# Neighbouring rows by a copy inside SBUF instead of two transposes: a four-layer residual kernel on one core of Trainium2

## The chip, the cores and the metric

The kernel runs on one core of one Trainium2 chip. The core has five engines, each with its own instruction queue: TensorE (PE in the profile; its weight loads are PEld), VectorE (DVE), ScalarE (ACT), GpSimd (POOL) and SyncE (SP). SP computes nothing here; it issues the DMA transfers. Engines wait for each other, and for transfers, through semaphores. The metric is device microseconds (us) of one execution; the result of a kernel is the median of its runs.

## The reference

The input x has 128 examples of 128 rows and 512 features (float32). Four layers follow, and each adds its result to x. All depend on per-example numbers (a mask kind, a language, three factors, a category).

```python
# layer 0: attention pooling with a mask per example
x = x + _L0_cond_ref(x, W1, b1, v, itok_B_0_2)
# layer 1: adapter with the language's weights, then a layer norm
x = x + _L1_cond_ref(x, itok_B_0_8, W1, b1, W2, b2, gamma, beta)
# layer 2: y is x after layer 1
yp_x = jnp.pad(y, ((0, 0), (0, 0), (1, 1)), mode='reflect')
lap_x = (yp_x[:, :, :-2] - 2.0 * y + yp_x[:, :, 2:]) / (dx * dx)
yp_y = jnp.pad(y, ((0, 0), (1, 1), (0, 0)), mode='reflect')
lap_y = (yp_y[:, :-2, :] - 2.0 * y + yp_y[:, 2:, :]) / (dy * dy)
du_dt = zX * lap_x + zY * lap_y + zR * y * (1.0 - y)      # factors of the example
x = x + du_dt
# layer 3: one 512x512 matrix per category
x = x + einsum('bsd,bdh->bsh', x, W[cat]) + b[cat][:, None, :]
```

The change touches layer 2. For each value it needs the neighbouring rows (`lap_y`) and the neighbouring features (`lap_x`), reflected at the edges.

## The kernel before, in words

One example is one tile of work: 128 rows on 128 partitions, 512 features along the row. Layers 0 and 1 run in this layout. For layer 2 the example is turned, because layer 3 needs the features on the partitions: partition p then holds features 4p to 4p + 3, as four chunks of 128 rows. In this layout

- the neighbouring rows of a value lie beside it on the same partition;
- the neighbouring features of chunks 1 and 2, and one neighbour each of chunks 0 and 3, lie in another chunk of the same partition;
- the feature before chunk 0 is chunk 3 of partition p - 1, and the feature after chunk 3 is chunk 0 of partition p + 1. These two are called the outer planes.

`y_transpose` (L514) turns the example by four TensorE transposes into `tr_y` (L524) and makes the two outer planes by two more, shifted by one feature, into `tr_e` (L528). `planes` (L530) copies all six into one SBUF tile `yT` of six planes with a border column at each side: the four inner ones (L534), the outer two (L535), the border columns (L536). `neighbours` (L545, GpSimd) adds the rows above and below into `ud`; `side_neighbours` (L553, GpSimd) adds the planes to the left and right into `lr`; `own` (L538, ScalarE), `diffuse_own`, `diffuse_rows` and `diffuse_columns` (L562 to L577, VectorE) put the layer together, the last of them into `x3T`. Layer 3 multiplies the four chunks of `x3T` with the category's matrix `w` (`project`, L599 to L606) into `po`; `finish` (L617) adds the bias row `b`, and `store` (L620) writes the example out. The `+ x` of layer 3 is an identity added to `w` by GpSimd (`residual`, L593).

Nothing is scheduled by a tool: every engine's order is written out by hand. `plan` (L626) is one iteration of the main loop (L717): each entry names a piece of work and an offset, and iteration i runs it for example i + offset. So one iteration works on some eight examples at once, each at another layer: `y_transpose` at offset -3, `project` at -4, `finish` and `store` at -5, `category` (which loads `w`, 1 MB) at -1, `residual` at -2. The first five iterations are replaced by `ramp` (L679), the same pieces in an order of their own. Examples 0 to 7 (`EARLY`) take another way through layer 0.

Transfers: SP issues eight in an iteration, in this order: the load of `w` (L582), the store (L621), the bias row `b` (L588), four block loads for a later example (L98), a load of `x` (L84). Each transfer counts up one of eight completion semaphores, taken in turn, and an instruction that issues a transfer first waits until the earlier transfers of its semaphore, the last of them eight issues back, have landed. Besides, the load of `w` waits for the buffer that TensorE read last, and the store for `finish`.

PSUM has eight banks: one for the turned example (`ps_tr`, tag `tr`), four for small tiles (`ps_sm`, tag `sm`: tr_e, pTp, sc, h, zh), two for `pool`, one for `po`.

Of the kernel before, what the change touches and what calls it, by code (L numbers as in the profile page):

```python
# [9 lines left out]
F32 = mybir.dt.float32  # L10
# [3 lines left out]
ALU = mybir.AluOpType  # L14
PSUM = bass.MemoryType.PSUM

P = 128
# [5 lines left out]
def kernel(  # L23
# [27 lines left out]
    nc = tc.nc  # L51
    B, S, D = x.shape
# [3 lines left out]
    NC = D // P  # L56
# [6 lines left out]
    one = ctx.enter_context(tc.tile_pool(name="one", bufs=1))  # L63
    two = ctx.enter_context(tc.tile_pool(name="two", bufs=2))
    outp = ctx.enter_context(tc.tile_pool(name="outp", bufs=4))
    ps_tr = ctx.enter_context(tc.tile_pool(name="ps_tr", bufs=1, space=PSUM))
    ps_sm = ctx.enter_context(tc.tile_pool(name="ps_sm", bufs=4, space=PSUM))
    ps_big = ctx.enter_context(tc.tile_pool(name="ps_big", bufs=2, space=PSUM))
    ps_out = ctx.enter_context(tc.tile_pool(name="ps_out", bufs=1, space=PSUM))

# [1 line left out]
    xt, w3t, b3t = {}, {}, {}  # L72
    st = [dict() for _ in range(B)]
# [2 lines left out]


    EARLY = 8
    R = 32
    Q = P // R  # L80

# [10 lines left out]
    def load_blocks(b):  # L92

        if b < EARLY:
            return
# [76 lines left out]
    zx = const.tile([P, B], F32, name="zx")  # L172
# [108 lines left out]
    def column(t, b):  # L281
        return t[:, b : b + 1]
# [11 lines left out]
    def turn(b):  # L294
        if b < EARLY:
            return
# [217 lines left out]
    def y_transpose(b):  # L514

        s = st[b]  # L520
        yp = s["yp"]
        s["yT"] = ps_tr.tile([P, NC, S], F32, tag="tr", name=f"tr_y_{b}")
        for c in range(NC):
            nc.tensor.transpose(s["yT"][:, c, :], yp[:, c + 1 : c + 2 + D - NC : NC], ident)  # L524
        s["outer"] = ps_sm.tile([P, 2, S], F32, tag="sm", name=f"tr_e_{b}")

        for i, at in ((1, NC + 1), (0, 0)):
            nc.tensor.transpose(s["outer"][:, i, :], yp[:, at : at + D - NC + 1 : NC], ident)  # L528

    def planes(b):  # L530
        s = st[b]
        s["planes"] = two.tile([P, NC + 2, S + 2], F32, tag="yT", name=f"yT_{b}")
        inner = s["planes"][:, 1 : NC + 1, :]
        nc.scalar.copy(inner[:, :, 1 : S + 1], s["yT"])  # L534
        nc.scalar.copy(s["planes"][:, 0 : NC + 2 : NC + 1, 1 : S + 1], s["outer"])  # L535
        nc.scalar.copy(inner[:, :, 0 : S + 2 : S + 1], inner[:, :, 2 : S : S - 3])  # L536

    def own(b):  # L538
        s = st[b]
# [10 lines left out]
            s["ud"], planes[:, 1 : NC + 1, 0:S], planes[:, 1 : NC + 1, 2 : S + 2]  # L550
        )

    def side_neighbours(b):  # L553
        s = st[b]
        planes = s["planes"]
        s["lr"] = one.tile([P, NC, S], F32, tag="lr", name=f"lr_{b}")
        nc.gpsimd.tensor_add(  # L557
            s["lr"], planes[:, 0:NC, 1 : S + 1], planes[:, 2 : NC + 2, 1 : S + 1]
        )


    def diffuse_own(b):  # L562
# [3 lines left out]
    def diffuse_rows(b):  # L566
# [2 lines left out]
            s["yT"], s["ud"], column(zy, b), s["yT"], ALU.mult, ALU.add  # L569
        )  # L570

    def diffuse_columns(b):
        s = st[b]
        s["x3T"] = two.tile([P, NC, S], F32, tag="x3T", name=f"x3T_{b}")
        nc.vector.scalar_tensor_tensor(  # L575
            s["x3T"], s["lr"], column(zx, b), s["yT"], ALU.mult, ALU.add
        )  # L577

    def category(b):
        st[b]["cat"] = index(nc.sync, 2, b, C - 1)  # L580
# [17 lines left out]

    def project(b, chunks):  # L599
        s = st[b]  # L600
        if 0 in chunks:
            s["po"] = ps_out.tile([S, D], F32, tag="po", name=f"po_{b}")
        for c in chunks:
            nc.tensor.matmul(  # L604
                s["po"], s["x3T"][:, c, :], w3t[b][:, c, :], start=(c == 0), stop=(c == NC - 1)
            )  # L606

    def project_first(b):
        project(b, [0])

    def project_middle(b):
        project(b, [1, 2])

    def project_last(b):
        project(b, [3])
# [4 lines left out]
    def store(b):  # L620
# [17 lines left out]
        (-1, mix_copy),  # L638
        (-4, project_first),
        (-2, adapter_bias),  # L640
        (-2, mean),
        (-3, planes),
        (-3, neighbours),
        (-2, statistics),
        (0, scores),
# [33 lines left out]
    ramp = """  # L679
        pe_index.1 act_index.0 pe_index.2 pe_index.3 turn_first.0 act_index.2 fetch_ids.2  # L680
        act_index.1 turn_first.1 act_index.4 act_index.3 act_index.5 load_x.2 early_weights.2
        act_index.6 first_products.0 fetch_ids.0 pe_index.0 load_w2.0 load_w2.2 first_products.1
        load_x.3 fetch_b1.0 row_at.0 hidden_bias.0 hidden.0 row_at.1 row_at.2 row_at.3
        row_by.vb.0 early_weights.3 row_by.vo.1 score.0 row_by.ab.2 turn_first.2 load_w2.4
        row_by.ab.3 load_w2.6 hidden_bias.1 mask_at.0 row_by.ab.5 masked.0 row_by.ao.4 load_w2.8
        scores.0 category.0 row_by.ab.6 mask_at.1 least.0 mask_at.2 mask_at.3 row_by.ab.8
        mask_at.5 row_by.vb.7 load_x.4 mask_at.4 row_by.ao.9 row_by.ab.10 row_by.ao.11
        row_by.ab.12 fetch_factors.0 row_by.ao.13 exps.0 row_by.ab.14 category.1 early_weights.4
        shares.0 weights.0 row_by.ao.15 mix_transpose.0 row_by.vb.16 hidden.1 row_by.vb.17
        mix_copy.0 pooled.0 score.1 masked.1 row_by.vs.20 scores.1 row_by.as.18 pooled_copy.0  # L690
        row_by.ao.19 first_products.2 least.1 residual.0 load_x.5 exps.1 hidden_bias.2
        turn_first.3 row_by.vo.21 row_by.as.22 row_by.vs.23 hidden.2 early_weights.5 adapter.0
        shares.1 row_by.ao.26 load_w1.0 row_by.as.24 adapter_bias.0 mean.0 row_by.vs.25
        weights.1 turn_first.4 factors.0 row_by.vo.29 mix_transpose.1 mix_copy.1 statistics.0
        row_by.as.28 pooled.1 residual.1 row_by.ao.27 score.2 load_x.6 first_products.3 masked.2
        pooled_copy.1 deviation.0 hidden_bias.3 category.2 load_w1.1 with_beta.0 centred.0
        early_weights.6 adapter.1 adapter_bias.1 mean.1 with_beta.1 hidden.3 turn_first.5 norm.0
        load_x.7 first_products.4 edges.0 scores.2 least.2 y_transpose.0 statistics.1 exps.2
        deviation.1 shares.2 weights.2 first_products.5 planes.0 score.3 centred.1 masked.3
        neighbours.0 own.0 norm.1 mix_transpose.2 scores.3 mix_copy.2 early_weights.7 least.3  # L700
        diffuse_own.0 pooled.2 load_w1.7 hidden_bias.4 exps.3 shares.3 side_neighbours.0 edges.1
        y_transpose.1 diffuse_rows.0 pooled_copy.2 adapter.2 weights.3 planes.1 with_beta.2
        diffuse_columns.0 project_first.0 mix_transpose.3 adapter_bias.2 hidden.4 neighbours.1
        category_row.0 mix_copy.3 load_w1.2 own.1 mean.2 project_middle.0 load_w1.3
        side_neighbours.1 load_x.8 statistics.2 category.3 deviation.2 pooled.3 load_w0.0
        score.4 diffuse_own.1 masked.4 centred.2 scores.4 pooled_copy.3 project_last.0 least.4
        norm.2 exps.4 with_beta.3 residual.2 diffuse_rows.1 edges.2 category_row.1 load_w1.6
        shares.4 load_w1.5 load_w1.8 weights.4 load_w1.9 load_w1.10 diffuse_columns.1 load_w1.11
        load_w1.12 load_w1.4 load_w1.13 load_w1.14 load_w1.15
    """  # L710
    done = set()
    for part in ramp.split():
# [48 lines left out]
```

## Time and profile before

| | |
|---|---|
| median of 3 runs | 1078.78 us (1078.53 to 1078.95) |
| the profiled execution's own time | 1078.29 us |
| its span (first to last instruction) | 1076.4 us, 19,485 instructions |
| granted TensorE clock | 0.994 of full |
| DMA, mean over the span | 256 GB/s, 275.97 MB in 152,646 packets |
| share of the 16 DMA engines that SP's queue kept busy | 78.3% |
| 128x512 `lr` on GpSimd (L557) | 128 times, 1280 ns |
| 128x512 `x3T` on VectorE (L575) | 128 times, 747 ns |
| transpose into tr_e (L528) | 256 times |
| copy of tr_e on ScalarE (L535) | 128 times, 392 ns |

Busy time is the time in which an engine executes; its share of the span says how full the engine is. The chain of waits is followed back from the last instruction: at each step to whatever released it, or to the instruction before it on its engine. A wait row names who waited, for whom, the total, how often and the longest. "To landing" is the time from a transfer's issue to the moment when its last part has arrived.

### The profile page before, as it was taken

What the parts mean: (1) busy time and instruction counts of PE and PEld (TensorE: products, weight loads), DVE (VectorE), ACT (ScalarE), POOL (GpSimd) and SP (SyncE); (2) the same over time, 40 slices, a digit from 0 to 9 for tenths busy, and PEclk for the clock granted to TensorE, in tenths of its full rate; (3) what the DMA queues carried; (4) which work ended last, traced back from release to release, by engine and by line L of the source; (5) the groups of instructions that cost most, each with busy time, mean ns of one, the idle gap of its engine ahead of it and who ended that gap; (6) DMA issues with size and microseconds to landing.
All of it is one profiled execution on the core that took longest, in us unless ns stands there. A gap on an engine that the chain in (4) does not pass through costs nothing.

```text
span 1076.4 us, 19485 instructions
## 1 busy us (share of the span) xinstructions
PE 1053.2 (98%) x3966; PEld 642.8 (60%) x3966; DVE 885.9 (82%) x2070; ACT 666.3 (62%) x2062; POOL 775.9 (72%) x921
## 2 busy tenths in 40 slices
PE   6889999999999999999999999999999999999997
PEld 4655665666666666666656656656656666566653
DVE  3578888888888888888888888888888888888885
ACT  4656666566566566666666666666665665665652
POOL 2557777777777777777777777777777777777775
PEclk8999999999999999999999999999999999999999
DMA  8789888787787877887788887887877887878853
GB/s 290 213 218 315 254 277 260 254 273 258 259 271 254 266 267 250 269 268 249 269 268 249 271 266 248 272 268 247 277 260 253 273 256 263 270 252 265 267 185 115
DMA packets 152646, 275.97 MB, mean 256 GB/s; under 512 B 16689, under 2 KB 84532, under 8 KB 136146
## 3 DMA queue, kind: packets, MB, share of 16 engines
q1 hardware_dynamic: 152326, 274.60, 78.3%
q8 instruction: 35, 0.57, 0.2%
q14 instruction: 81, 0.66, 0.2%
q10 hardware_dynamic: 204, 0.13, 0.1%
HBM read 241.11 MB, written 33.55 MB: 255 GB/s over the span
## 4 chain that ended last, share of the span: by engine, by line
PE 95%; DVE 2%; ACT 1%; issue 1%; DMA 0%; POOL 0%; SPq 0%; DVEq 0%; POOLq 0%; ACTq 0%
PE po L604 40%; PE zh L330 21%; PE pool L420 10%; PE pool L444 10%; PE tr_y L524 6%; PE tr_e L528 3%; PE h L422 3%; PE pTp L410 1%; PE sc L380 1%; PE row L274 0%; DVE tr_y L568 0%; DVE x3T L575 0%; DMA x<-in_x_dram 0%; PE tr_x L291 0%; ACT b_tab L277 0%
## 5 line engine op out<-in xcount | busy, mean ns | idle before, releaser
L604 PE MATMUL po<-w,x3T 128*128 128x512 f32 x1024 | 482.4, 594 | 1.3 <-issue 1.3
L604 PEld LDWEIGHTS po<-w,x3T 128*128 128x128 f32 x1024 | 175.3, 191 | 126.3 <-issue 126.3
L330 PEld LDWEIGHTS zh<-w,xT 128*128 128x128 f32 x1088 | 199.7, 193 | 78.7 <-issue 29.9
L330 PE MATMUL zh<-w,xT 128*128 128x256 f32 (+1 forms) x1088 | 244.4, 370 | 0.9 <-ACT yT L535 0.9
L597 POOL TENSOR_TENSOR w<-w,ident 128x512 f32<-128x512 f32 x128 | 198.3, 1549 | 10.8 <-DMA w<-in_L_cond_W_dram 10.8
L549 POOL TENSOR_TENSOR ud<-yT 128x512 f32<-128x512 f32 x128 | 133.0, 1039 | 100.9 <-ACT yT L536 100.9
L348 ACT ACTIVATE zh<-zh 128x128 f32<-128x128 f32 x128 | 33.6, 262 | 219.3 <-PE zh L330 207.9
L436 POOL TENSOR_TENSOR x<-x,beta_tab 128x512 f32<-128x512 f32 x128 | 162.9, 1273 | 4.5 <-ACT x L431 3.5
L557 POOL TENSOR_TENSOR lr<-yT 128x512 f32<-128x512 f32 x128 | 163.8, 1280 | 0.0
L469 POOL TENSOR_SCALAR mean<-total 128x1 f32<-128x1 f32 x128 | 28.4, 222 | 147.1 <-DVE pool L456 138.1
L420 PE MATMUL pool<-x,pT 128*128 128x512 f32 x256 | 132.7, 600 | 0.8 <-DVE gamma_tab L277 0.4
L444 PE MATMUL pool<-w_tab,h1s 128*128 x256 | 130.8, 593 | 0.0
L415 ACT COPY pT<-pTp 128x128 f32<-128x128 f32 x128 | 34.0, 266 | 143.2 <-PE pTp L410 143.2
L524 PEld LDWEIGHTS tr_y<-ident,y 128*128 128x128 f32 x512 | 80.9, 204 | 66.2 <-issue 62.2
L494 DVE SCALAR_TENSOR_TENSOR pool<-pool,mean,gamma_tab 128x512 f32<-128x512 f32 x128 | 97.0, 758 | 25.4 <-ACT y L476 24.9
L385 DVE TENSOR_REDUCE least<-sc 128x1 f32<-128x128 f32 x128 | 37.3, 292 | 90.4 <-PE sc L380 90.4
L575 DVE SCALAR_TENSOR_TENSOR x3T<-lr,zx,tr_y 128x512 f32<-128x512 f32 x128 | 95.6, 747 | 13.5 <-DVE tr_y L568 0.5
L541 ACT ACTIVATE own<-tr_y,cy,nzr 128x512 f32<-128x512 f32 x128 | 99.1, 774 | 0.0
L618 DVE TENSOR_TENSOR b<-po,b 128x512 f32<-128x512 f32 x128 | 88.5, 691 | 11.8 <-PE po L604 3.8
L568 DVE SCALAR_TENSOR_TENSOR tr_y<-ud,zy,tr_y 128x512 f32<-128x512 f32 x128 | 95.7, 748 | 0.1
L506 DVE SCALAR_TENSOR_TENSOR y<-pool,rstd,x 128x512 f32<-128x512 f32 x128 | 95.7, 747 | 0.0
L456 DVE SCALAR_TENSOR_TENSOR pool<-pool,b_tab 128x512 f32<-128x512 f32 x128 | 88.7, 693 | 2.2 <-PE pool L444 2.0
(82 smaller groups left out, 1649.9 us busy)
## 6 DMA issues: line engine op xcount, KB each, us to landing
w<-in_L_cond_W_dram SPq DMA_DIRECT2D x128, 1024.0 KB, 5.2
x<-in_x_dram SPq DMA_DIRECT2D x128, 256.0 KB, 3.5
b<-in_L_cond_b_dram SPq DMA_DIRECT2D x128, 256.0 KB, 4.0
out_dram<-b SPq DMA_DIRECT2D x128, 256.0 KB, 2.8
blocks<-in_x_dram SPq DMA_DIRECT2D x480, 64.0 KB, 4.0
w_tab<-in_L_cond_W_dram SPq DMA_DIRECT2D x5, 512.0 KB, 5.6
w_tab<-in_L_cond_W_dram SPq DMA_DIRECT2D x16, 160.0 KB, 6.3
w<-in_L_cond_W_dram SPq DMA_DIRECT2D x9, 256.0 KB, 3.8
```

Source lines behind the costliest of these rows:

```text
L330: nc.tensor.matmul(s["zh"][:, part, :], s["xT"][:, c, :], w[:, c], start=(c == 0 and b < EARLY), stop=(c == NC - 1), skip_group_check=True,)
L420: nc.tensor.matmul(s["xx"], s["pT"], xt[b], start=True, stop=True)
L436: nc.gpsimd.tensor_add(s["x1"], s["x1"], beta_tab[:, ds(at, D)])
L444: nc.tensor.matmul(s["xx"], s["h1"], w2_tab[:, ds(s["pe_at"], D)], start=False, stop=True, skip_group_check=True,)
L494: nc.vector.scalar_tensor_tensor(s["xx"], s["xx"], s["mean"], gamma_tab[:, ds(s["dve_at"], D)], ALU.subtract, ALU.mult,)
L506: nc.vector.scalar_tensor_tensor(s["yp"][:, 1 : D + 1], s["xx"], s["rstd"], s["x1"], ALU.mult, ALU.add)
L524: nc.tensor.transpose(s["yT"][:, c, :], yp[:, c + 1 : c + 2 + D - NC : NC], ident)
L541: nc.scalar.activation(s["own"], s["yT"], AF.Identity, bias=column(cy, b), scale=column(nzr, b))
L549: nc.gpsimd.tensor_add(s["ud"], planes[:, 1 : NC + 1, 0:S], planes[:, 1 : NC + 1, 2 : S + 2])
L557: nc.gpsimd.tensor_add(s["lr"], planes[:, 0:NC, 1 : S + 1], planes[:, 2 : NC + 2, 1 : S + 1])
L597: nc.gpsimd.tensor_add(diag, diag, ident.unsqueeze(1).to_broadcast([P, NC, P]))
L604: nc.tensor.matmul(s["po"], s["x3T"][:, c, :], w3t[b][:, c, :], start=(c == 0), stop=(c == NC - 1))
```

## The change

The two shifted transposes are left out from the third example on (`BESIDE = 2`). The outer planes are copied from the neighbouring partitions by DMA, within SBUF, after `planes`: chunk 3 (plane NC) of partitions 0 to 126 goes to the plane before chunk 0 of partitions 1 to 127, and chunk 0 (plane 1) of partitions 1 to 127 to the plane after chunk 3 of partitions 0 to 126. Each of the two copies is split into 112 and 15 partitions, so there are four transfers, `fetch_beside`, issued by SP. ScalarE writes the two reflected edges (one partition each; the second as a block of 32, of which the last counts).

The side sum and `x3T` are each made in two halves: chunks 1 and 2, which need no outer plane, where they were made before; chunks 0 and 3 (`side_outer`, `columns_outer`) one iteration later, between `adapter_bias` and `mean`. `project` takes the chunks in the order 1, 2, 0, 3. The turned example in PSUM is thus needed longer and gets a second bank; the small tiles, of which tr_e is no more, have three instead of four. The ramp's order is somewhat changed.

SP's order in an iteration becomes: `w`, store, four fetches, `b`, four block loads, `x`: twelve transfers. With eight semaphores in turn, in one iteration `w` takes semaphore 6, the store 7, the fetches 0 to 3, `b` 4, the block loads 5, 6, 7 and 0, `x` 1, and the next `w` 2.

```diff
-    ps_tr = ctx.enter_context(tc.tile_pool(name="ps_tr", bufs=1, space=PSUM))
-    ps_sm = ctx.enter_context(tc.tile_pool(name="ps_sm", bufs=4, space=PSUM))
+    ps_tr = ctx.enter_context(tc.tile_pool(name="ps_tr", bufs=2, space=PSUM))
+    ps_sm = ctx.enter_context(tc.tile_pool(name="ps_sm", bufs=3, space=PSUM))
...
+    BESIDE = 2
...
             nc.tensor.transpose(s["yT"][:, c, :], yp[:, c + 1 : c + 2 + D - NC : NC], ident)
+        if b >= BESIDE:
+            return
         s["outer"] = ps_sm.tile([P, 2, S], F32, tag="sm", name=f"tr_e_{b}")
...
-        nc.scalar.copy(s["planes"][:, 0 : NC + 2 : NC + 1, 1 : S + 1], s["outer"])
+        if b < BESIDE:
+            nc.scalar.copy(s["planes"][:, 0 : NC + 2 : NC + 1, 1 : S + 1], s["outer"])
+        else:
+
+            nc.scalar.copy(s["planes"][0:1, 0, 1 : S + 1], s["yT"][0:1, 1, :])
+            nc.scalar.copy(
+                s["planes"][P - R : P, NC + 1, 1 : S + 1], s["yT"][P - R : P, NC - 2, :]
+            )
         nc.scalar.copy(inner[:, :, 0 : S + 2 : S + 1], inner[:, :, 2 : S : S - 3])
+
+    def fetch_beside(b):
+        if b < BESIDE:
+            return
+        planes = st[b]["planes"][:, :, 1 : S + 1]
+        for a, e in ((0, P - 16), (P - 16, P - 1)):
+            nc.sync.dma_start(planes[a + 1 : e + 1, 0, :], planes[a:e, NC, :])
+            nc.sync.dma_start(planes[a:e, NC + 1, :], planes[a + 1 : e + 1, 1, :])
...
+    def side(b, chunks):
+        s = st[b]
+        planes = s["planes"]
+        first, last, step = chunks
+        nc.gpsimd.tensor_add(
+            s["lr"][:, first : last + 1 : step, :],
+            planes[:, first : last + 1 : step, 1 : S + 1],
+            planes[:, first + 2 : last + 3 : step, 1 : S + 1],
+        )
+
     def side_neighbours(b):
...
+        st[b]["lr"] = one.tile([P, NC, S], F32, tag="lr", name=f"lr_{b}")
+        side(b, (0, NC - 1, 1) if b < BESIDE else (1, NC - 2, 1))
+
+    def side_outer(b):
+        if b >= BESIDE:
+            side(b, (0, NC - 1, NC - 1))
...
+    def columns(b, chunks):
+        s = st[b]
+        first, last, step = chunks
+        at = slice(first, last + 1, step)
+        nc.vector.scalar_tensor_tensor(
+            s["x3T"][:, at, :], s["lr"][:, at, :], column(zx, b), s["yT"][:, at, :],
+            ALU.mult, ALU.add,
+        )
+
     def diffuse_columns(b):
...
+        st[b]["x3T"] = two.tile([P, NC, S], F32, tag="x3T", name=f"x3T_{b}")
+        columns(b, (0, NC - 1, 1) if b < BESIDE else (1, NC - 2, 1))
+
+    def columns_outer(b):
+        if b >= BESIDE:
+            columns(b, (0, NC - 1, NC - 1))
...
-                s["po"], s["x3T"][:, c, :], w3t[b][:, c, :], start=(c == 0), stop=(c == NC - 1)
+                s["po"], s["x3T"][:, c, :], w3t[b][:, c, :], start=(c == 1), stop=(c == 3)
...
-        project(b, [0])
+        project(b, [1])
...
-        project(b, [1, 2])
+        project(b, [2, 0])
...
         (-2, adapter_bias),
+        (-4, side_outer),
+        (-4, columns_outer),
         (-2, mean),
         (-3, planes),
+        (-3, fetch_beside),
         (-3, neighbours),
...
```

## The prediction

> **What bounds the kernel now.** I read the page's busy times and its chain of waits first, then the chain in one middle iteration, then SP's timeline and waits over the same stretch, then the landing times of the weight load.
>
> ```profile
> PE 1053.2 (98%) x3966; PEld 642.8 (60%) x3966; DVE 885.9 (82%) x2070; ACT 666.3 (62%) x2062; POOL 775.9 (72%) x921
> PE 95%; DVE 2%; ACT 1%; issue 1%; DMA 0%; POOL 0%; SPq 0%; DVEq 0%; POOLq 0%; ACTq 0%
> ```
> The chain that ended last runs on TensorE for 95% of the span. One iteration of it:
> ```profile
> 507.25 2.58 PE po L604 x6
> 509.82 1.73 PE zh L330 x8
> 511.55 0.86 PE pool L444 x2
> 512.41 0.47 PE tr_y L524 x4
> 512.88 0.24 PE tr_e L528 x2
> 513.12 0.11 PE pTp L410
> 513.23 0.86 PE po L604 x2
> 514.09 0.11 PE sc L380
> 514.20 0.86 PE pool L420 x2
> 515.06 0.22 PE h L422 x2
> 515.28 0.43 PE po L604
> ```
> The pieces touch: no idle time from 507.25 to 515.28, a period of 8.03 us. From 81.31 to 1045.54 us the same chain repeats 120 times, 8.035 us each, and the tr_e piece that the change takes out is 0.24 us of each.
>
> SP, the queue that issues the transfers, in the same kind of stretch (start, duration, what):
> ```profile
> 501.91 0.36 SPq L582 DMA_DIRECT2D w<-in_L_cond_W_dram  x1
> 504.11 0.34 SPq L621 DMA_DIRECT2D out_dram<-b  x1
> 504.64 0.34 SPq L588 DMA_DIRECT2D b<-in_L_cond_b_dram  x1
> 505.03 1.97 SPq L98 DMA_DIRECT2D blocks<-in_x_dram  x4
> 507.05 0.43 SPq L84 DMA_DIRECT2D x<-in_x_dram  x1
> 509.95 0.36 SPq L582 DMA_DIRECT2D w<-in_L_cond_W_dram  x1
> ```
> Its two long waits over the run (us in total, times, longest):
> ```profile
> SPq L621 <- DVE b L618: 213.8, 116, 5.9
> SPq L582 <- PE po L604: 192.2, 118, 3.7
> ```
> And the landing times of the weight load L582 between 100 and 1000 us:
> ```profile
> DMA to landing us min/median/max: 4.7/5.2/6.2
> ```
> SP has about 3.5 us of slack in each iteration: 213.8/116 = 1.84 us at the store, 192.2/118 = 1.63 at the weight load, which lands 5.2 us after its issue. One more row of SP's waits matters, from the start of the run (18 to 24 us), where many transfers are open at once:
> ```profile
> SPq L126 <- DMA w<-in_L_cond_W_dram: 1.4, 1, 1.4
> ```
> Here SP stands still, with no buffer to wait for, until the transfer eight issues earlier has landed; it issues 0.02 us after that landing mark. So at most eight transfers of this queue are open. Before, an iteration issues exactly eight, each counter is reused a whole iteration later, and the rule costs nothing.
>
> **The change, part by part.**
> TensorE: two transposes less, 0.24 us, for 126 of 128 examples: 126 x 0.24 = 30.2 us. If nothing else came up, the period would be 8.035 - 0.24 = 7.80.
>
> ScalarE: one 128x256 copy (392 ns) goes, two of 128 elements come (266 ns each by the L350 row): +0.14 us. It is hidden: ACT idles 1.74 + 1.12 us per iteration before L348 and L415.
>
> VectorE: x3T in halves. 128x512 takes 747 ns and 128x128 of the same operation 343 ns (L405), so 1.05 ns an element and 0.21 fixed: two halves take 0.96, +0.21 us. DVE idles 0.72 + 0.17 us per iteration before L385 and L494; 0.24 of that goes with the shorter period, leaving 0.4. The outer half stands in the gap before L385. Without that cover it is 0.21 us an iteration, 26 us.
>
> GpSimd: the side sum in halves; half of 1280 ns, plus between nothing and a fixed 0.22 (the one-element row, L469): +0 to 0.44 us, against 1.09 + 0.79 us of idle time. Hidden.
>
> PSUM banks: four tenants on three sm banks. The longest held is zh (ACT 508.08 to DVE 512.5); its bank is wanted next at 515.1, so nothing waits. The second tr bank takes away the last iterations' waits of tr_y for x3T (0.84 + 0.42 + 2.00 us), and the last example's fetch, now exposed, costs between one landing (4.0, the blocks row) and nothing. I put ends and start at 0, with 3 us to either side.
>
> The new copies: 254 rows of 512 bytes. Four block loads (512 such rows) land 0.3 us apart, so these add some 0.55 us to the DMA engines, which are busy 78.3% of 8.035 = 6.3 us: room in 7.80. Their issue costs 0.34 to 0.49 us each (the store's and the blocks' rows), 1.4 to 2.0 us on SP. They wait for the planes (ACT L536 ends at 506.5), and b, the four blocks, x and the next w queue behind them. By issue time alone b moves from 504.64 to about 508.2, x to 510.6, w to 511.9 instead of 509.95: 1.9 us late, with its reader (POOL L597, at 519.0) still 1.9 us behind its landing. The fetch lands 2.8 us (store row) to 4.0 (blocks row) after its issue, at 511.8 at the latest; side_outer runs at about 512. So far all is hidden, and the sum is 1078.3 - 30.2 = 1048.
>
> A 64 KB block load lands after 4.0 us. The Trainium skill (DMA: Bandwidth & Descriptors, Rules for kernel authors) calls transfers under 64 KB mostly overhead, which speaks against four such copies; its Anatomy section gives a fixed 2.0 us (measured there for GpSimd's path). An estimate by it has a 57 KB copy landing 2.1 us after issue, and the sum stays 1048, since the copy is covered either way; the 4.0 us of the blocks row holds queueing.
>
> What is not hidden is the limit of eight. An iteration now issues twelve: w, store, four fetches, b, four blocks, x. The eighth after w is the second block load, the eighth after the store is the third. So there is a loop without any compute engine in it: w is issued; the store, right behind it in the same rings, lands after it; only then go the third and the fourth block load and x, and only then the next w. Its terms: w lands after 5.2 (4.7 to 6.2). The store's 256 KB follow at the 312 to 348 GB/s of the windows 502.8 to 507.1: +0.7, so 5.9. Lower bound for that term: the store lands on its own 2.8 us after issue, before w, and w's landing releases the second block load instead. Two block issues: 2 x 0.5 = 1.0, or 0.85 if the first, after a stand, takes 0.34. From x's issue to w's: 509.95 - 507.05 - 1.63 of waiting = 1.27. Sum 5.9 + 1.0 + 1.27 = 8.17, or 8.02; I take 8.15, the upper one, since late landings (the 6.2) have nothing to absorb them. The lower bound: 5.2 + three issues 1.5 + 1.27 = 7.97. All low, with w at 4.7: 7.3. High: w at 5.4 on average, a store 0.9 behind: 8.6.
>
> So SP's loop of 8.15 replaces TensorE's 8.035. It does not start at once: w may drift by the 3.2 us between its landing (507.1) and POOL's use of it (about 510.3), at 8.15 - 7.80 = 0.35 per iteration, so nine iterations still run at 7.80 and 3 us are saved. 1078.3 + 120 x (8.15 - 8.035) - 3 = 1089. The profiled run's own 1078.3 stands 0.5 below the median.
>
> **Rivals.**
> A, the forecast: the loop of transfers decides, 8.15, 1089 us; between 8.03 and 8.3, 1075 to 1107. For it: the stand in the ramp, and terms read from rows. Against: it misses the old period by 0.1 only.
> B, TensorE stays the bound: 1048. The loop must close in under 7.80, so w and store must land 0.35 us sooner than summed. For: w is now issued closely behind x, so its first reads may not start cold. Against: w's median is 5.2 with little in front of it.
> C, the loop decides but is short, 7.80 to 8.0: 1050 to 1072. For: the lower bound of 7.97. This is the store landing beside w rather than after it.
> D, the copies themselves are slow: x waits for the second fetch and the fourth block load for the first; if rows copied inside SBUF took three times those of the blocks, the two would land some 1.6 us behind the store instead of 0.5, x 0.6 us later: 8.75, about 1160.
> That the transposes are not taken out is no rival: the program has 252 fewer on TensorE.
>
> **How the numbers follow.** A 0.57, B 0.14, C 0.19, D 0.10. A change under 0.2% (2.2 us) can't be told from none. Slower: D and nearly 0.5 of A, 0.59; same: 0.08, out of A; faster: B, C, 0.33. The range leaves out most of D and half of B: 1050 to 1110; A's own is 1075 to 1107.
>
> **What would show it.** Right: SP waiting at the block loads for transfers (w and store), a TensorE period near 8.15 with idle pieces, and GpSimd or DVE waiting for the fetch or for w. Tr_e gone and the tr_y, pTp pieces touching shows the first step. Wrong: a gapless TensorE chain at 7.80, SP still waiting for PE at L582's load, or a w landing below 4.9. If DVE shows no idle time at all, its 0.21 us was the bound.

## The result and the profile after

| | before | after |
|---|---|---|
| median | 1078.65 us (1077.39 to 1078.95, 4 runs) | 1290.12 us (1286.81 to 1297.46, 4 runs) |
| ratio | | 1.197, 95% interval 1.192 to 1.203 |
| span of the profiled execution | 1076.4 us | 1285.0 us |
| granted TensorE clock | 0.994 | 0.979 |
| period of the main loop, mean from 300 to 1000 us | 8.04 us | 9.85 us |

The change makes the kernel a fifth slower. 1.81 us more in each of some 120 periods is 217 us, a little more than the 211 us of difference: the whole of it is the period of the main loop. The page's busy times and its chain of waits of the changed kernel:

```profile
PE 1092.2 (85%) x3714; PEld 614.9 (48%) x3714; DVE 878.6 (68%) x2197; ACT 716.9 (56%) x2187; POOL 796.0 (62%) x1047
...
DMA 42%; SPq 22%; POOL 10%; issue 7%; DVE 4%; PE 3%; POOLq 2%; ACT 2%; ACTq 2%; DVEq 1%
DMA yT<-yT 35%; SPq L556 11%; SPq L555 10%; DMA b<-in_L_cond_b_dram 6%; POOL lr L577 6%; DVE least L388 3%; POOL rstd L493 2%; ACTq L90 2%; POOLq L90 2%; POOL ve L492 2%; PE po L645 2%; ACT sc L394 1%; DVEq L497 1%; DMA out_dram<-b 0%; ACT 
...
L577 POOL TENSOR_TENSOR lr<-yT 128x256 f32<-128x256 f32 (+1 forms) x254 | 186.5, 734 | 399.2 <-DMA yT<-yT 399.1
...
w<-in_L_cond_W_dram SPq DMA_DIRECT2D x128, 1024.0 KB, 6.5
...
yT<-yT SPq DMA_DIRECT2D x252, 56.0 KB, 5.9
yT<-yT SPq DMA_DIRECT2D x252, 7.5 KB, 4.6
```

TensorE held 95% of the chain before and holds 3% now. Its place is taken by transfers (DMA) and by SP's queue, the one that issues them (SPq). The copies inside SBUF (`yT<-yT`) are the largest part of the chain, and GpSimd stands idle 399.1 us for them, 3.2 us an example. It is tempting to stop here and say that the copies are slow. SP's own waits (us in total, times, longest) say something else:

```profile
SPq L101 <- DMA w<-in_L_cond_W_dram: 113.7, 111, 3.2
SPq L101 <- DMA out_dram<-b: 37.7, 112, 1.6
```

L101 is the block load. It needs neither `w` nor the store; it waits for them because its completion semaphore is the one that they hold, eight issues back. And SP's timeline over one iteration (start, duration, what; a row of several transfers includes the waits between them):

```profile
513.94 0.36 SPq L623 DMA_DIRECT2D w<-in_L_cond_W_dram  x1
514.40 0.38 SPq L662 DMA_DIRECT2D out_dram<-b  x1
514.89 0.59 SPq L555 DMA_DIRECT2D yT<-yT  x1
515.53 0.92 SPq L556 DMA_DIRECT2D yT<-yT  x1
516.50 0.90 SPq L555 DMA_DIRECT2D yT<-yT  x1
517.44 0.82 SPq L556 DMA_DIRECT2D yT<-yT  x1
518.46 0.38 SPq L629 DMA_DIRECT2D b<-in_L_cond_b_dram  x1
518.89 2.10 SPq L101 DMA_DIRECT2D blocks<-in_x_dram  x4
521.03 0.43 SPq L87 DMA_DIRECT2D x<-in_x_dram  x1
522.51 0.36 SPq L623 DMA_DIRECT2D w<-in_L_cond_W_dram  x1
```

SP has no slack left: from one `w` to the next it issues transfers or waits for them. Of its waits for compute engines in the loop, the largest is 36.3 us over the run, 0.6 us at a time at most (L555 for GpSimd). The four copies take 3.23 us of issue here. The landing marks of the trace, as medians over the middle of the run and counted from the issue of `w`: `w` lands at 6.54, the second block load goes out at 6.55; the store lands at 7.17, the third block load goes out at 7.19; `x` goes out at 8.19 and the next `w` at 9.74 (taken pair by pair, this last gap has a median of 1.48). From 300 to 1000 us the second block load follows the landing of `w` by less than 0.1 us in 70 of 71 iterations.

SP's waits at the block loads, 113.7 for `w` and 37.7 for the store, come to 151.4 us over the run, which is less than the 211 that the change costs. An estimate by subtraction, 1290 - 151 = 1139, is still above the kernel before: the four copies keep SP issuing for so long that the shortest of these periods, 8.42 us, is longer than the old 8.04.

Two theories were put to the test. LOOP: with twelve transfers in an iteration and eight semaphores, SP waits for the iteration's own `w` and store, and what is copied doesn't matter. COPIES: the copies inside SBUF are slow themselves, or what waits for them is late.

### The profile page after: what moved, and what is told of

Same layout as the page of the kernel before. It is cut to its first block, busy times and chain, and to the rows that moved or that the text cites. A ratio compares the mean times of both kernels' runs of the same rounds, so it can differ in the third digit from the quotient of the medians.

```text
span 1285.0 us, 20364 instructions
## 1 busy us (share of the span) xinstructions
PE 1092.2 (85%) x3714; PEld 614.9 (48%) x3714; DVE 878.6 (68%) x2197; ACT 716.9 (56%) x2187; POOL 796.0 (62%) x1047
## 4 chain that ended last, share of the span: by engine, by line
DMA 42%; SPq 22%; POOL 10%; issue 7%; DVE 4%; PE 3%; POOLq 2%; ACT 2%; ACTq 2%; DVEq 1%
DMA yT<-yT 35%; SPq L556 11%; SPq L555 10%; DMA b<-in_L_cond_b_dram 6%; POOL lr L577 6%; DVE least L388 3%; POOL rstd L493 2%; ACTq L90 2%; POOLq L90 2%; POOL ve L492 2%; PE po L645 2%; ACT sc L394 1%; DVEq L497 1%; DMA out_dram<-b 0%; ACT yT L539 0%
## 5 line engine op out<-in xcount | busy, mean ns | idle before, releaser
L645 PE MATMUL po<-w,x3T 128*128 128x512 f32 x1024 | 528.7, 626 | 172.7 <-DVE x3T L607 121.3
L577 POOL TENSOR_TENSOR lr<-yT 128x256 f32<-128x256 f32 (+1 forms) x254 | 186.5, 734 | 399.2 <-DMA yT<-yT 399.1
L645 PEld LDWEIGHTS po<-w,x3T 128*128 128x128 f32 x1024 | 168.0, 192 | 356.4 <-DVE x3T L607 207.4
L607 DVE SCALAR_TENSOR_TENSOR x3T<-lr,zx,tr_y 128x256 f32<-128x256 f32 (+1 forms) x254 | 122.5, 482 | 303.1 <-POOL lr L577 290.0
L333 PE MATMUL zh<-w,xT 128*128 128x256 f32 (+1 forms) x1088 | 252.2, 378 | 0.0
L333 PEld LDWEIGHTS zh<-w,xT 128*128 128x128 f32 x1088 | 206.9, 200 | 86.5 <-ACT zh L320 48.2
L394 ACT ACTIVATE sc<-sc,least 128x128 f32<-128x128 f32 x128 | 43.7, 342 | 260.4 <-DVE least L388 260.2
L479 ACT ACTIVATE y<-pool,total 128x512 f32<-128x512 f32 x128 | 88.2, 689 | 26.4 <-DVE pool L459 24.9
L497 DVE SCALAR_TENSOR_TENSOR pool<-pool,mean,gamma_tab 128x512 f32<-128x512 f32 x128 | 92.9, 726 | 2.8 <-ACT y L479 2.7
```

The lines of the kernel that those rows point to most:

```text
L333: nc.tensor.matmul(s["zh"][:, part, :], s["xT"][:, c, :], w[:, c], start=(c == 0 and b < EARLY), stop=(c == NC - 1), skip_group_check=True,)
L497: nc.vector.scalar_tensor_tensor(s["xx"], s["xx"], s["mean"], gamma_tab[:, ds(s["dve_at"], D)], ALU.subtract, ALU.mult,)
L577: nc.gpsimd.tensor_add(s["lr"][:, first : last + 1 : step, :], planes[:, first : last + 1 : step, 1 : S + 1], planes[:, first + 2 : last + ...
L607: nc.vector.scalar_tensor_tensor(s["x3T"][:, at, :], s["lr"][:, at, :], column(zx, b), s["yT"][:, at, :], ALU.mult, ALU.add,)
L645: nc.tensor.matmul(s["po"], s["x3T"][:, c, :], w3t[b][:, c, :], start=(c == 1), stop=(c == 3))
```

## The experiments

Line numbers in the diffs are left out; `aside` is a spare tile that nobody reads. "`w` lands" is the median of the landing marks in the middle of the run, from issue to the last part. A time without a range is that of a single run. In e1, e2, e3 and e5 ScalarE fills the places that no transfer reaches with values of another chunk, so these kernels leave out part of the computation; that part of their edits is not shown.

### One cause at a time: e1 to e4

**e1_sixteen.** The two transfers of 15 partitions become transfers of 16.

```diff
-        for a, e in ((0, P - 16), (P - 16, P - 1)):
-            nc.sync.dma_start(planes[a + 1 : e + 1, 0, :], planes[a:e, NC, :])
-            nc.sync.dma_start(planes[a:e, NC + 1, :], planes[a + 1 : e + 1, 1, :])
+        a, e = 0, P - 16
+        nc.sync.dma_start(planes[a + 1 : e + 1, 0, :], planes[a:e, NC, :])
+        nc.sync.dma_start(planes[a:e, NC + 1, :], planes[a + 1 : e + 1, 1, :])
+        nc.sync.dma_start(aside[0:16, :], planes[P - 17 : P - 1, NC, :])
+        nc.sync.dma_start(aside[16:32, :], planes[P - 16 : P, 1, :])
```

> The changed kernel with the two transfers of 15 partitions replaced by two of 16 partitions that go to a spare tile; the last 15 partitions of the outer planes are filled by ScalarE with wrong values. Still twelve transfers an iteration. Theory LOOP (eight open transfers, twelve issued; the weights and the store behind them land late whatever the copies are): still near 1290, 1250 to 1300. Theory FIFTEEN (a transfer over 15 engines unbalances the 16 and delays the next weight load to 6.5 us): weights land after 5.5, the loop is 5.5 + 0.7 + 1.0 + 1.5 = 8.7, 1150 to 1180.

1269.14 us, in LOOP's range; FIFTEEN falls. The odd number of partitions is worth 21 of the 211 us and no more: their issue takes 0.6 us each instead of 0.8 to 0.9. The period stays at 9.6, and `w` lands at 6.81.

**e2_no_fifteen.** The 15-partition transfers are left out, ten in an iteration.

```diff
-        for a, e in ((0, P - 16), (P - 16, P - 1)):
+        for a, e in ((0, P - 16),):
```

> The changed kernel without the two transfers of 15 partitions (filled by ScalarE, wrong values): ten transfers an iteration, so the eighth after the weight load is the fourth block load and the eighth after the store is the load of x. Theory LOOP: 5.5 + 0.7 + 1.5 = 7.7, under TensorE's 7.80: 1045 to 1065. Theory COPIES (copies inside SBUF hold up the weight load, 6.5 us and more): 6.5 + 0.7 + 1.5 = 8.7, 1150 to 1180.

1160.72 us. This was nearer to the number of COPIES than to LOOP's, which was a miss of LOOP's price: with ten transfers `w` releases the fourth block load and the store releases `x`, so the loop is still closed (6.70 for `w`, 7.47 for the store, then `x` and the next `w`, 8.8 in all), and `w` did not land at the 5.2 that LOOP had been priced with.

**e3_no_fetch.** No fetch at all, eight transfers.

```diff
-        for a, e in ((0, P - 16), (P - 16, P - 1)):
+        for a, e in ():
```

> The changed kernel without any fetch (outer planes filled by ScalarE, wrong values): eight transfers. Theories LOOP, COPIES and FIFTEEN: TensorE is the bound at 7.80, 1045 to 1052. Theory HALVES (the split sums and x3T, a half one iteration later, or three small PSUM banks, cost time themselves): over 1070.

1046.53 us (1045.03 to 1048.07), 0.970 of the kernel before (0.969 to 0.972). TensorE has the chain again and `w` lands early; the chain of waits and the landing row of e3:

```profile
PE 95%; DVE 1%; DMA 1%; POOL 1%; ACT 1%; SPq 1%; issue 0%; POOLq 0%; DVEq 0%
...
w<-in_L_cond_W_dram SPq DMA_DIRECT2D x128, 1024.0 KB, 5.1
```

So all of the change but the four transfers is worth what two transposes cost, and the halves and the lost PSUM bank cost nothing.

**e4_before_plus_four.** The kernel *before*, with four loads of 16 x 512 bytes from HBM behind the store. Nobody waits for them; there is no copy inside SBUF.

```diff
+    def four_more(b):
+        for i in range(4):
+            nc.sync.dma_start(aside[i * 16 : (i + 1) * 16, :], x[b, 0:16, i * P : (i + 1) * P])
...
         (-3, planes),
+        (-3, four_more),
         (-3, neighbours),
```

> The kernel before with four loads of 16 x 512 bytes from HBM into a spare tile, put where the fetches stand, read by nobody. Twelve transfers, no copy inside SBUF, no wait for the planes. Theory LOOP: weights 5.2 to 5.5, store +0.7, block issues and x 1.0, to the next weights 1.3 to 1.5: 8.2 to 8.7, 1095 to 1160. Theories COPIES and FIFTEEN: no change, 1078.

1250.03 us: 32 KB an example that nobody reads make the old kernel 16% slower. SP's waits are those of the changed kernel (L98 is the block load here):

```profile
SPq L98 <- DMA w<-in_L_cond_W_dram: 248.2, 119, 4.0
SPq L98 <- DMA out_dram<-b: 41.9, 115, 1.8
```

LOOP is shown, with a price above the one that it had: 1250 where 1089 or so would follow from the prediction's terms. `w` lands at 6.45, with no copy inside SBUF about.

### The copies without the loop: e5

Two 112-partition fetches, and the block loads made two: eight transfers.

```diff
-        for q in range(Q):
+        for h in range(2):
             nc.sync.dma_start(
-                st[b]["blocks"][q * R : (q + 1) * R, :].rearrange("r (i e) -> r i e", i=Q),
-                x[b, :, q * P : (q + 1) * P].rearrange("(i r) e -> r i e", r=R),
+                st[b]["blocks"][h * 64 : (h + 1) * 64, :].rearrange("r (i e) -> r i e", i=2),
+                x[b, :, h * 256 : (h + 1) * 256].rearrange("(i r) e -> r i e", r=64),
...
-        for a, e in ((0, P - 16), (P - 16, P - 1)):
+        for a, e in ((0, P - 16),):
```

> Kernel after with the two 15-partition transfers left out and the four block loads of 32 partitions made two of 64 (same bytes; the table of blocks is filled in another order, so the output is not the reference's). The two fetches of 112 partitions stay: eight transfers per example, as before the change. Rows to build on: 1290 with twelve, 1160.7 with ten and these same two fetches, 1046.5 with eight and no fetch. LOOP (the number of transfers sets the wait for a counter; what is copied does not matter): with eight no issue waits for the example's own w, TensorE is the bound again, 1045 to 1065, period 7.8 to 7.95, and L101 does not wait for w. COPIES (the transfers between partitions delay what depends on them or slow the queue): the two fetches are still there, 1100 to 1165.

1057.94 us, against 1160.72 with the same copies among ten transfers. The chain of waits of e5:

```profile
PE 84%; DMA 5%; POOL 2%; DVE 1%; issue 1%; ACT 1%; SPq 0%; POOLq 0%; DVEq 0%
```

COPIES falls as the reason for the 211 us: two of the copies, with the larger block loads, cost the 11 us between this kernel and e3. But LOOP is too simple where it says that what is copied doesn't matter. `w` lands at 7.70 here, and 60 times the next `w` waits for it (48.8 us in all); with eight transfers there is nearly a whole period before that costs anything.

### The fetch from another queue: e6, e10, e11

**e6_gpsimd.** Two copies of 127 partitions, issued by GpSimd.

```diff
-        for a, e in ((0, P - 16), (P - 16, P - 1)):
-            nc.sync.dma_start(planes[a + 1 : e + 1, 0, :], planes[a:e, NC, :])
-            nc.sync.dma_start(planes[a:e, NC + 1, :], planes[a + 1 : e + 1, 1, :])
+        nc.gpsimd.dma_start(planes[1:P, 0, :], planes[0 : P - 1, NC, :])
+        nc.gpsimd.dma_start(planes[0 : P - 1, NC + 1, :], planes[1:P, 1, :])
```

> Kernel after, whole computation, with the fetch made of two transfers of 127 partitions issued by GpSimd, whose queue has its own completion counters; SP is back to eight transfers. LOOP: w lands about 5.1 to 5.3 after its issue, no block load waits for it, 1046 to 1060 as long as GpSimd's own work stays under TensorE's period. GpSimd is busy 796/128 = 6.2 per example in the profile of after, so there is 1.6 left per example for two issues: under 0.8 each the kernel stays at 1046 to 1060; at 1.0 to 1.5 each GpSimd is the bound at 8.2 to 9.2, 1100 to 1220. COPIES: the copies are the same ones between partitions, 1200 or more, with GpSimd's and VectorE's waits for them as in after. TensorE ends within 2 per cent of kernel e3's 1046 only if LOOP holds and the issue is cheap.

1124.05 us (1123.61 to 1126.48), 1.042 of the kernel before (1.040 to 1.044). `w` lands at 5.31 and SP no longer waits for it; LOOP is right so far. But the kernel is not at 1046, and GpSimd is not full either (84%). GpSimd's timeline shows where it went:

```profile
602.22 0.22 POOL L472 TENSOR_SCALAR mean<-total 128x1 f32<-128x1 f32 x1 [0.84 <-DVE pool L459]
602.42 0.63 POOL L554 DMA_DIRECT2D yT<-yT  x1
603.05 0.54 POOL L555 DMA_DIRECT2D yT<-yT  x1
603.60 1.06 POOL L568 TENSOR_TENSOR ud<-yT 128x512 f32<-128x512 f32 x1
604.75 0.18 POOL L492 TENSOR_SCALAR ve<-squares 128x1 f32<-128x1 f32 x1
605.02 0.57 POOL L493 TENSOR_TENSOR rstd<-ve,neg_half 128x1 f32<-128x1 f32 x1
```

The two issues stand between `mean` and `rstd`, on which VectorE waits. With `ud` they hold `rstd` back by 2.2 us, and 0.84 us of GpSimd's idle time lies ahead of `mean`, where it is of no use.

**e10_gpsimd_early.** The fetch goes ahead of `mean`.

```diff
-        (-2, mean),
         (-3, planes),
         (-3, fetch_beside),
+        (-2, mean),
```

> Kernel e6 (fetch by two transfers of 127 partitions issued by GpSimd, 1124) with the fetch moved ahead of the mean in GpSimd's order, whole computation. In e6 GpSimd is busy 941/128 = 7.4 per example and not full, the period is 8.33, and the chain of waits runs through VectorE's sum, GpSimd's mean, the two issues (0.63 + 0.54), ud (1.06), rstd and back to VectorE. QUEUE ORDER (what costs is that the issues and ud stand between mean and rstd): 0.84 of the 1.17 of issue falls into the idle stretch ahead of the mean, rstd is ready 0.3 to 0.6 earlier, period 7.8 to 8.05, 1050 to 1085. GPSIMD FULL (its busy time is the limit): no change, 1115 to 1130.

1126.78 us (1124.49 to 1127.77): a miss for QUEUE ORDER as it was placed here. The fetch has to wait for ScalarE's `planes` (0.91 and 0.41 us idle ahead of it in two iterations of GpSimd's timeline), which end after the sum is there, so `mean` moved back by 1 us and gave up what `rstd` won.

**e11_gpsimd_ud_later.** `ud` goes behind `rstd` instead.

```diff
-        (-3, neighbours),
         (-2, statistics),
...
         (-2, deviation),
+        (-3, neighbours),
```

> Kernel e6 with ud (the 1.06 us sum of the rows above and below) moved behind rstd in GpSimd's order, whole computation. QUEUE ORDER: ud leaves the chain from VectorE's sum to rstd, 1.06 less there, while VectorE needs ud only behind y; the chain would be 7.3 and TensorE's 7.8 decides, 1046 to 1070, the first of these kernels with the fetch that is below the kernel before. GPSIMD FULL: no change, 1115 to 1130.

1060.51 us (1058.62 to 1062.06), 0.983 of the kernel before (0.981 to 0.985). It is the whole computation and beats both kernels. GpSimd is as busy as in e6, so GPSIMD FULL falls: what cost 64 us was one instruction of 1.06 us in the wrong place. The busy times of e11:

```profile
PE 1027.6 (97%) x3714; PEld 610.0 (58%) x3714; DVE 937.3 (88%) x2197; ACT 695.3 (66%) x2187; POOL 935.8 (88%) x1299
```

### Why `w` lands at 6.5: e7, e8, e9, e12, e13, e14, e15

What the loop costs beyond the prediction is mostly the landing of `w`: 6.45 to 6.8 in the changed kernel, e1, e2 and e4, 5.2 in the kernel before. All runs of this part but e15 build on e4.

**e7_store_last.** The store goes behind `x`.

```diff
-        (-5, store),
...
         (FIRST, load_x),
+        (-5, store),
```

> Kernel before with four added loads of 16 x 512 B that nobody reads (the same as in e4: twelve transfers, 1250.0, w landing 6.46 after its issue), and the store moved from behind w to behind the load of x, the last of the example. Computation whole. STORE-DELAYS-W (w lands at 6.5 in place of 5.2 because the store is issued 0.4 behind it and shares its engines): w lands at 5.1 to 5.6. SELF (it lands late for another reason, such as the loads issued just ahead of it, or the waiting itself): w lands at 6.2 to 6.8. Either way the store no longer stands in the loop between w and the next w (0.75), so the period is e4's 9.44 less 0.5 to 0.8 by SELF, 8.6 to 8.9, 1140 to 1185; by STORE-DELAYS-W another 1.0 to 1.3 less, 7.8 to 8.0, 1070 to 1090 with TensorE as the bound.

1250.48 us, `w` at 6.87: STORE-DELAYS-W falls. SELF had the landing nearly right (just above its 6.8), and not the time: the store left one place in the loop and took another, between `x` and `w`, whose gap went from 1.26 to 1.75. In this kernel it is thus the store that stands right ahead of `w`, by 1.22.

**e8_four_before_w.** The four loads go between `x` and `w`.

```diff
         (FIRST, load_x),
+        (-3, four_more),
...
-        (-3, four_more),
```

> Kernel e4 (the kernel before and four added loads of 16 x 512 B that nobody reads, twelve transfers, 1250.0) with the four loads moved from behind the store to between x and the next w. Computation whole. What it tells apart is why w lands 6.5 after its issue in the kernels whose loop closes, and 5.2 in the kernel before. AHEAD (x and the last block loads, issued within 1.6 ahead of w, are still on the engines; in the kernel before x is 2.9 ahead): x is now some 3 ahead of w, so w lands at 5.1 to 5.5; period = w's landing, then four issues held by w's and the store's landings (0.7 + 3 x 0.45) and about 0.9 to the next w, 8.1 to 8.5, 1085 to 1130. BEHIND (what is issued within 2 us behind w shares the engines with it; in the kernel before nothing comes for 2.2): store, b and the blocks come at once behind w, which lands at 6.3 to 7.0, period 9.3 to 10, 1230 to 1310.

1190.2 us, `w` at 5.45 although the store goes out 0.46 and the rest at once behind it. That is AHEAD. Its time was 60 us too low: the four loads waited not only for `w` and the store but also for `b` (85.4 us over the run), which I had not counted.

**e9_pause** and **e12_long_pause.** Two and five register loads between `w` and the store.

```diff
     def store(b):
+        for _ in range(2):
+            index(nc.sync, 1, b, L - 1)
         nc.sync.dma_start(out[b], b3t[b])
```

> Kernel e4 with two loads of a register (about 1 each, from the gap of 0.9 to 1.1 that one such load makes between x and w in the timeline of SP's queue) between w and the store, and nothing else: a pause of some 2 us behind w, more work for SP. Computation whole. BEHIND: nothing is issued for 2.2 behind w, so it lands at 5.1 to 5.5; the loop is 5.3 + store's landing 0.7 + block issue 0.45 + x and the next w 1.5 to 2, 8.0 to 8.6, or what SP itself needs for the issues behind the pause (2.2 + 7 x 0.45 + 0.9 + 2.0 = 8.3): 1085 to 1140, faster than e4 by 100 or more although work was added. AHEAD: w lands at 6.3 to 6.8 as in e4, period 9.4 or more, 1240 to 1290.

1226.4 us, `w` at 6.35. Two loads made a pause of 1.14, not 2, so the store went out 1.60 behind `w`, and AHEAD's time was missed too: the pause cost nothing, and the time was 24 us below e4's (one run of each). BEHIND was not tried cleanly; hence e12:

> Kernel e9 with five register loads behind w in place of two. In e9 each took 0.57 (the store went out 1.60 behind w, against 0.46 in e4), so the pause was shorter than meant and w landed at 6.35; here the store goes out about 3.3 behind w. Computation whole. The kernels so far: w lands at 5.1 to 5.3 where nothing follows for over 2 us (before, e3, e6, e11, whatever is still under way ahead of it), at 5.45 where transfers follow at once but x had gone out 4.9 ahead (e8), and at 6.35 to 6.9 where x is close ahead and transfers follow within 1.6 (after, e2, e4, e7, e9). BOTH (lateness needs transfers close ahead and close behind): w lands at 5.0 to 5.5 although x is 1.2 to 1.6 ahead. AHEAD ALONE: 6.2 to 6.7. The time tells little, since SP's own issues fill the period: 3.3 to the store, 4.7 from there to x in e9 without its waits, 1.25 to the next w, 9.0 to 9.4, 1190 to 1240 by BOTH, without a wait for w; by AHEAD ALONE the same or more.

1292.84 us, above BOTH's times. `w` lands at 6.54 with nothing behind it for 3.3 us, so BOTH falls, AHEAD ALONE has the landing, and nothing that follows `w` is needed to make it late. First one iteration of SP's timeline of e12, then its landing row:

```profile
788.10 0.43 SPq L84 DMA_DIRECT2D x<-in_x_dram  x1
789.35 0.36 SPq L587 DMA_DIRECT2D w<-in_L_cond_W_dram  x1
792.62 0.34 SPq L628 DMA_DIRECT2D out_dram<-b  x1
```

`w` goes out 1.25 behind `x` here, and the store 3.27 behind `w`. The landing row, with KB and the median us to landing:

```profile
w<-in_L_cond_W_dram SPq DMA_DIRECT2D x128, 1024.0 KB, 6.5
```

What was left is how far `w` goes out behind `x`: 2.88 us in the kernel before, 2.38 in e11, 2.23 in e6, and 1.2 to 1.5 in after, e1, e2, e4, e9 and e12, where it lands late. (e7 has 1.75, with the store between, and e5 1.71.)

**e13_gap_ahead** and **e14_small_gap.** Two register loads, and one, between `x` and `w`.

```diff
     def category(b):
...
         w3t[b] = w3p.tile([P, NC, D], F32, tag="w3", name=f"w3_{b}")
+        for _ in range(2):
+            index(nc.sync, 1, b, L - 1)
```

> Kernel e4 with two register loads (0.57 each, from e9) between x and the next w: w goes out 2.4 behind x in place of 1.27. Nothing else changes, and computation is whole. DISTANCE (w lands late because it goes out under some 2 us behind x; before 2.87, e3 2.7, e11 2.4, e6 2.2: 5.1 to 5.3; after 1.55, e4 1.27, e9 and e12 1.25: 6.35 to 6.55): w lands at 5.0 to 5.5, and the pause of 1.14 is paid back by it: period 9.2 to 9.6, 1225 to 1265, no more than e4's 1250 within 2 per cent. CLOSED LOOP (w lands late in every kernel in which SP never waits for the engines, whatever its distance): 6.3 to 6.9, the pause adds its 1.14 to the period, 10.4 to 10.8, 1370 to 1420.

> Kernel e4 with one such register load between x and the next w: 1.84 apart. Computation whole. DISTANCE: w lands between, at 5.2 to 6.2, period 9.2 to 9.7, 1225 to 1280. CLOSED LOOP: w at 6.3 to 6.9, period 9.9 to 10.2, 1310 to 1345.

e13: 1256.27 us, `w` at 5.39. e14: 1195.63 us, `w` at 5.36. DISTANCE in both, and e14 went below its range: the landing doesn't slide from 6.45 to 5.4 as the gap grows, it is all there at 1.84. With one instruction more, e4 is 54 us faster (one run of each). In e4 itself, the seven iterations in which `w` happens to go out about 1.6 behind `x` land at 5.41, without the added instruction. One iteration of SP's timeline in e4, and one in e14:

```profile
708.60 0.43 SPq L84 DMA_DIRECT2D x<-in_x_dram  x1
709.87 0.36 SPq L587 DMA_DIRECT2D w<-in_L_cond_W_dram  x1
710.33 0.38 SPq L626 DMA_DIRECT2D out_dram<-b  x1
```

```profile
706.64 0.43 SPq L84 DMA_DIRECT2D x<-in_x_dram  x1
708.46 0.36 SPq L589 DMA_DIRECT2D w<-in_L_cond_W_dram  x1
708.92 0.39 SPq L628 DMA_DIRECT2D out_dram<-b  x1
```

The store is as close behind as in e4; only `x` is further ahead, 1.82 instead of 1.27. These two `w` land after 6.10 and 5.37. And the landing row of e14:

```profile
w<-in_L_cond_W_dram SPq DMA_DIRECT2D x128, 1024.0 KB, 5.4
```

**e15_after_gap.** The edit of e14 (one load) in the changed kernel.

> The changed kernel (1290.1) with one register load (0.57) between x and the next w, as in e14; nothing else, computation whole. There w goes out 1.55 behind x and lands at 6.54. DISTANCE: at 2.0 to 2.2 it lands at 5.2 to 5.6, the loop is 5.4 + 0.65 (store) + 0.5 + 0.5 (block issues) + 2.1 = 9.15 at most, 1185 to 1225: 70 to 100 less than the changed kernel, though an instruction was added. If the lateness in the changed kernel is of another kind than in e4 (its copies inside SBUF): w stays at 6.3 to 6.9 and the time is 1290 or more.

1287.24 us: a miss for DISTANCE in the time, while the landing, 5.67 in place of 6.54, is just above its 5.6. `w` goes out 2.06 behind `x`. SP's waits in e15 show where the gain went:

```profile
SPq L101 <- DMA w<-in_L_cond_W_dram: 65.0, 94, 2.4
SPq L555 <- POOL lr L577: 32.9, 65, 1.3
SPq L101 <- DMA out_dram<-b: 31.9, 101, 0.6
```

The two waits for `w` and the store are 96.9 us instead of 151.4, which is 54.5 less. The added load costs 0.58 in each of some 120 iterations, 70 us, and the first fetch now waits 32.9 us for GpSimd. Most iterations are shorter (median period 9.39 instead of 9.69). But in a quarter of them `w` still lands after 6.24 (in e14 after 5.45), up to 8.6, so that the mean period stays at 9.85.

**What was still under way.** One thing in the traces orders these runs better than the gap does. The packets of `w` have 8192 bytes each, and the first of them comes about 1 us after the issue (0.99 in the kernel before, 1.10 in e4). Leave them out, and ask how busy the 16 DMA engines were with other packets from 0.5 to 1.0 us after the issue of `w`, as a mean from 300 to 1000 us of the run. In before, e3, e8, e13, e14 and e15 it is 0 to 14%, and `w` lands at 5.1 to 5.7. In after, e1, e2, e4, e5, e7, e9 and e12 it is 41% or more, and `w` lands at 6.4 to 7.7; this includes e5 and e7, which the gap puts in the wrong place. Between the iterations of the changed kernel it is the same: under 10% `w` lands at 5.63 (median of 11), up to 40% at 5.91 (48), up to 70% at 7.02 (34), above at 7.31 (23). For the two `w` of e4 and e14 shown above, the rows of that half microsecond end with the share of the DMA engines and their GB/s:

```profile
710.37:710.87 0.50, 0.50 (x3) 0.30 (x2) 0.41 (x3) 0.16 (x1) 0.11 (x1) 1.00 0.94 361
...
708.96:709.46 0.50, 0.50 (x2) 0.19 (x1) 0.50 (x2) 0.50 (x2) 0.50 (x2) 1.00 0.00 0
```

So `w` lands late where the engines are not yet through with what SP issued ahead of it. Busy engines alone are not it: in e6, e10 and e11, where GpSimd's copies are among the other packets, 40 to 72% go with 5.2 to 5.3. No run was made for this reading alone, and why such a short rest costs `w` more than a microsecond stays open.

## Why the prediction was wrong

Step by step, as it was put:

- *TensorE: 0.24 us a period, 1048 if nothing else came up.* Right: e3 measured 1046.53, with TensorE the bound.
- *ScalarE, VectorE, GpSimd's halves, PSUM hidden.* Right, by the same run: none of them shows in it.
- *The limit of eight closes a loop without a compute engine.* Right, and shown from two sides: e4 makes the loop without the copies, e5 and e6 make the copies without the loop. This gave the direction. It is not the whole of the time: SP's waits for `w` and the store come to 151 us, and the kernel is 211 us slower than before and 244 us slower than e3.
- *The loop's length, 8.15.* **This is the step that failed.** It measured 9.74, of which 1.57 are above the sum of 8.17. `w` lands after 6.54 instead of 5.2: +1.34. The store 0.63 behind it instead of 0.7: -0.07. The two block issues 1.02 instead of 1.0. From `x` to the next `w` 1.55 instead of 1.27: +0.28.
- Inside it, what was wrong is the pair of two numbers. The 5.2 was read where `w` goes out 2.88 behind `x`; the 1.27 is the same gap with TensorE's wait of 1.63 taken out. The sum used both, but they exclude each other: e4 has the 1.26 and the landing of 6.45, e14 has a gap of 1.84 and the landing of 5.36. What goes with the difference is whether SP's earlier transfers are still being moved when `w` starts. The bounds did not hold it either, since the highest (5.4 for `w`) came from rows of the same kernel. Two smaller slips changed little: 256 KB at 312 to 348 GB/s is 0.75 to 0.84 us, not 0.7 (0.63 was measured), and GpSimd uses `w` at 510.98 (L597), not at about 510.3.
- *Issue of the copies, 0.34 to 0.49 us each.* Too small: 0.59, 0.95, 0.90 and 0.82, 3.26 in all instead of 1.4 to 2.0. The bound came from transfers to and from HBM in a kernel where SP had slack; here a copy of 112 partitions took longer to issue, and one of 15 as well. This is the second term that failed, since it was put at nothing, as hidden: SP gets to the second block load only 5.4 to 5.5 us behind `w`, so a landing at 5.2 alone would hardly have made the loop 8.15 either; the shortest period is 8.42.
- *The fetch lands 2.8 to 4.0 after its issue, hidden.* Wrong in size, 5.9 and 4.6; the fetches land about a microsecond behind `w`, which went out ahead of them, and GpSimd waits 3.2 us an example for them. In e5, where the loop is open and two of the copies are left, all of it is worth 11 us.
- *Rival B (TensorE stays the bound) and C (a short loop).* Both fell. B's ground, that `w` close behind `x` may start sooner, is the reverse of what e4 and e14 show. *D (the copies themselves slow, `x` held by the second fetch, about 1160).* It came nearest in time by accident: `x` goes out right behind the fourth block load, never held by the fetch.
- *A `w` landing below 4.9 would show it wrong.* The mistake lay on the other side of 5.2, which the text left without a sign.

The rule that was weighed, the Trainium skill's that transfers under 64 KB are mostly overhead (DMA: Bandwidth & Descriptors, Rules for kernel authors), points the right way, but the runs find the overhead in another place: nobody reads e4's four 8 KB loads, so their slowness delays nothing, and they cost 172 us by their number.

The same section says that spreading transfers over several issuing engines doesn't help bandwidth and only saves time of issue. e6 and e11 show a second gain, where SP's waits for `w` go away: in the trace of e6 SP's transfers count up eight semaphores and GpSimd's copies eight others.

## What to carry to other kernels

Count the transfers of an iteration against the completion semaphores of their queue: once there are more, a transfer waits for one of its own iteration, and four that nobody needs can cost more than the work that they replace. A latency read in a kernel with slack belongs to the spacing in which it was read; before it goes into the sum for a closed loop, ask what will be issued just ahead of it there, and whether the DMA engines will be through with it. Add up the issues of the queue as well: here, by the estimate above, they alone came to more than the old period. When work moves to another queue, look at what it stands in front of: with the same two issues on GpSimd the kernel takes 1124 or 1061 us, by the place of one instruction.

## What the runs showed of the hardware

- A 1 MB load of SP's queue lands after 5.1 to 5.7 us where the DMA engines are 0 to 14% busy with other packets from 0.5 to 1.0 us after its issue (before, e3, e8, e13, e14, e15), and after 6.4 to 7.7 where they are 41% busy or more (after, e1, e2, e4, e5, e7, e9, e12). With copies issued by GpSimd among these packets it lands after 5.2 to 5.3 (e6, e10, e11). Why was not found.
- In e4 and its variants a gap of 1.26 us behind the 256 KB load of `x` goes with 6.45 us, gaps of 1.84 and 2.40 go with 5.36 and 5.39 (e14, e13). What is issued behind `w` doesn't decide it: all at once in e8 (5.45), nothing for 3.3 us in e12 (6.54).
- A kernel can thus get faster by an instruction that does nothing: e14 is 54 us below e4, one run of each.
- The median issue of a copy inside SBUF takes SP 0.6 to 0.95 us (after), and GpSimd 0.63 and 0.54 us (e6). A load from HBM mostly takes SP 0.3 to 0.5 us, but 0.72 for the third of e4's added loads and 0.92 for the first block load of e8, so not all of it belongs to the kind of transfer.
